# Attention weights of three query groups in four transposed by DMA, through one ring of three buffers

## The chip, the core and the metric

The kernel runs on one NeuronCore of a Trainium2 chip. The metric is the device time of one execution in microseconds (us), of which the median over several runs is given. The core's engines work through queues of their own and wait for each other by semaphores: PE (TensorE, matrix products), DVE (VectorE), ACT (ScalarE), POOL (GpSimd), and SP, which here only issues DMA transfers. PE's weight loads are a row of their own in the profile, PEld.

## What is computed

The input x is 4 sequences of 1024 tokens with 256 channels, in float32. Four layers are added to it in turn, each on its layer-normalized input: a linear recurrent layer, a sparse feed-forward layer with softmax gates and top-32 choices, an attention layer with 8 heads, and the same feed-forward layer once more. The change lies in the attention layer:

```python
q = (x @ Wq.T).reshape(b, t, N_HEADS, HEAD_DIM)           # 8 heads of 64
kv_latent = x @ Wkv_down.T                                # 64 wide, shared by the heads
k = (kv_latent @ Wk_up.T).reshape(b, t, N_HEADS, HEAD_DIM)
v = (kv_latent @ Wv_up.T).reshape(b, t, N_HEADS, HEAD_DIM)
scores = jnp.einsum('bqhd,bkhd->bhqk', q, k) * HEAD_DIM ** (-0.5)
attn = jax.nn.softmax(scores, axis=-1)
out = jnp.einsum('bhqk,bkhd->bqhd', attn, v)
return out.reshape(b, t, N_HEADS * HEAD_DIM) @ Wo.T
```

The key weights are folded into the queries and the value weights into the output, so that the kernel's attention works on the 64-wide latent itself.

## The kernel before

The program has three stages. The first, up to about 377 us, holds the recurrent layer, the head of the first feed-forward layer and its first eight tiles. The second, from about 377 to 1305 us, is the attention over all four sequences, with the other 24 tiles of the first feed-forward layer woven into it. The third is the second feed-forward layer.

In the second stage the method `heads` runs over units. A unit is a group of 128 queries (`q`, four of them in a block `nb` of 512) of a pair of heads (`g`, four pairs); there are 4 x 2 x 4 x 4 = 128 units, and each has two halves `j`, one for each head of the pair. I call one such half a "half": 256 in all. For each half,

- PE computes the scores of 128 queries against 1024 keys as four products (line 887) into one of two `sc` buffers in PSUM;
- DVE negates and copies them into one of four `pr` buffers, with the row's extreme value `nm` (line 893, and a small line 895 for units that go by DMA);
- ACT takes the exponentials in place and their sum `ssum` (line 896).

The weights then have to be turned, so that keys lie on the partitions. There are two ways. A unit "by DMA" (`by_dma`, before: `q` is 0 or 2) is split in two float16 parts in a `pd` buffer: ACT casts (line 899), POOL subtracts the cast from the original (line 900), and SP issues one DMA transpose of both parts (line 901) into a `d` buffer. A unit "by PE" (`q` is 1 or 3) takes eight PE transposes for each half (line 907) in two PSUM tiles, which ACT copies into a `p` buffer (line 912; in the last sequence DVE copies the first of the two, line 910).

Later `values_sum` multiplies the turned weights with the latent values (line 932): a unit by DMA takes 24 float16 products for each half (high and low parts of both factors), 48 in all, and a unit by PE 8 float32 products for each half, 16 in all, each of which the profile records as two. DVE makes the reciprocals `rs` of the sums (line 926), POOL spreads them over 64 columns for each head in `rows` (line 928), PE transposes that (line 940), ACT copies it (line 942) and DVE multiplies (line 943). Sums of units by DMA wait in the list `late`, those by PE in `pending`; both are emptied at the end of each sequence. The rings are: two `d` buffers for each half, one `p` buffer for each half, two `pd`, two `rows`.

The order on each engine is not that of the Python text alone. `merge` weaves the steps of the side work (queries, output products, the feed-forward tiles and others) between halves by due numbers written by hand, and then a scheduler orders each engine's queue, so that a sum can stand several halves behind the place where it was written. Nothing is reordered at run time: an instruction that waits holds up all that stand behind it on its engine.

A feed-forward tile of the second stage (`tile` with `fine=True`) writes exponentials into `ex` (ACT, line 615), finds the 32 largest of each of two gates by four rounds of top-8 search on DVE (line 674), and uses `ex` last in a POOL product with `xg` (line 658). It loads a precomputed product `full` by an SP transfer (line 599).

Of the kernel before, what the change touches and what calls it, by code (L numbers as in the profile page):

```python
# [10 lines left out]
F32 = mybir.dt.float32  # L11
# [3 lines left out]
F16 = mybir.dt.float16  # L15
# [6 lines left out]
P = 128  # L22
B = 4
T = 1024
D = 256
KD = D // P
TPB = T // P
# [3 lines left out]
HD = 64  # L31
PAIRS = HEADS // 2
# [147 lines left out]
class Banks:  # L180


    def __init__(self, pool, bufs):
        self.pool, self.bufs = pool, bufs
# [303 lines left out]
class Ffn:  # L488
# [100 lines left out]
    def tile(self, i, sp, psum, tags, out=None, fast=False, parts=None, tt=None, fine=False):  # L589


        nc, w = self.nc, self.w
        pool = nc.vector if fast else nc.gpsimd
        x = self.x[i]
        blk, tk = i // 4, slice((i % 4) * P, (i % 4 + 1) * P)
        full = None
        if blk in self.full:
            full = sp.tile([P, D], F32, tag="full", name="full")
            nc.sync.dma_start(full, self.full[blk][:, i % 4, :])
        pl = psum.tile([P, 2, D], tags[0], "pl")  # L600
        self.logits_product(pl, i)


        nr = TOPK // 8
        m8 = sp.tile([P, 2, nr, 8], F32, tag="m8", name="m8")
        e8 = sp.tile([P, 2, 8], F32, tag="e8", name="e8")
        nm = sp.tile([P, 2], F32, tag="nm", name="nm")
        ssum = sp.tile([P, 2], F32, tag="ssum", name="ssum")
        ex = sp.tile([P, 2, D], F32, tag="ex", name="ex")
        wk = sp.tile([P, 2, D], F32, tag="wk", name="wk", **({"bufs": 1} if fine else {}))  # L610
        for s in range(2):
            self.ordered(nc.vector.max, m8[:, s, 0, :], pl[:, s, :])
        nc.gpsimd.tensor_scalar(nm, m8[:, :, 0, 0], -1.0, 0.0, ALU.mult, ALU.add)
        for s in range(2):
            nc.scalar.activation(  # L615
                ex[:, s, :], pl[:, s, :], AF.Exp, bias=nm[:, s : s + 1], accum_out=ssum[:, s : s + 1]
            )
            self.last_exp = nc.scalar.activation(e8[:, s, :], m8[:, s, 0, :], AF.Exp, bias=nm[:, s : s + 1]).ins
        yield
        for r in range(nr):  # L620
            for s in range(2 if r else 0):
                self.ordered(nc.vector.max, m8[:, s, r, :], wk[:, s, :])
            for s in range(2):
                v, k = (wk, m8[:, s, r, :]) if r else (ex, e8[:, s, :])
                self.ordered(nc.vector.match_replace, wk[:, s, :], k, v[:, s, :], 0.0)
            if fine and r < nr - 1:
                yield
        pool.tensor_tensor(ex, ex, wk, ALU.subtract)  # L628
        rs = sp.tile([P, 2], F32, tag="rs", name="rs")
        nc.vector.reciprocal(rs, ssum)  # L630
        yield

        q = i % 4
        norm = self.norm[blk]
        if full is not None:
            nc.vector.scalar_tensor_tensor(full, full, rs[:, 0:1], ex[:, 0, :], ALU.mult, ALU.mult)
            ob = full
        else:
            if tt is not None:
                pf = psum.tile([P, D], tags[2], "pf")  # L640
                self.full_product(pf, tt, q)
            else:
                xn = sp.tile([P, D], F32, tag="fxn", name="fxn")
                with self.tc.issue_after(self.convolved):
                    nc.scalar.activation(
                        xn, x, AF.Identity, bias=norm[:, 1, q : q + 1], scale=norm[:, 0, q : q + 1]
                    )
                pf = self.product(sp, psum, tags, xn, None, parts)
            ob = sp.tile([P, D], F32, tag="ob", name="ob")
            nc.scalar.mul(ob, pf, rs[:, 0:1])  # L650
            pool.tensor_tensor(ob, ob, ex[:, 0, :], ALU.mult)
        yield

        xg = sp.tile([P, D], F32, tag="xg", name="xg", bufs=2)
        sc = sp.tile([P, 2], F32, tag="sc", name="sc")
        pool.tensor_scalar(sc, norm[:, :, q], rs[:, 1:2], 0.0, ALU.mult, ALU.add)
        nc.scalar.activation(xg, x, AF.Identity, bias=sc[:, 1:2], scale=sc[:, 0:1])
        pool.tensor_tensor(xg, xg, ex[:, 1, :], ALU.mult)
        nc.gpsimd.tensor_tensor(x, x, ob, ALU.add)
        pi = self.product(sp, psum, tags, xg, w.bias, parts)  # L660
        if out is None or fast:
            nc.vector.tensor_tensor(x, x, pi, ALU.add)
        else:
            yi = sp.tile([P, D], F32, tag="yi", name="yi")
            nc.scalar.copy(yi, pi)
            nc.gpsimd.tensor_tensor(x, x, yi, ALU.add)
        if out is not None:
            nc.sync.dma_start(out[i // 4][:, i % 4, :], x)
        yield
# [104 lines left out]
class Attention:  # L774
    def __init__(self, tc, x, ident, ident64, wqk, wvo, wd, sp, wp):
        self.nc, self.x, self.ident, self.ident64 = tc.nc, x, ident, ident64
        self.wqk, self.wvo, self.wd, self.sp, self.wp = wqk, wvo, wd, sp, wp
        self.hp = None
        self.k, self.xnt, self.qs, self.on = {}, {}, {}, {}

        self.sident = wp.tile([HD, HD], F32R, tag="sident", name="sident")
# [75 lines left out]
    def heads(self, b, psum):  # L857
# [2 lines left out]

        nc, sp, wp = self.nc, self.sp, self.hp
        kh, kl, la, lb = self.k[b]
        late, pending = [], []
        for nb, g, q in (
            (nb, g, q)
            for nb in range(2)
            for g in range(PAIRS)
            for q in ((0, 2, 1, 3) if b == B - 1 and nb and g == PAIRS - 1 else range(4))
        ):
            by_dma = q % 2 == 0  # L870
            if g == 0:
                self.on[b, nb, q] = wp.tile([P, PAIRS, P], F32, tag=f"on{q}", name=f"on{q}")
            qs = self.qs[b, nb, g]
            ssum = sp.tile([P, 2], F32, tag="ssum", name="ssum", bufs=4)
            if by_dma:
                pts = [wp.tile([P, 2 * TPB, P], F16, tag=f"d{j}", name=f"d{j}", bufs=2) for j in range(2)]
                parts = ((0, lb[0]), (TPB, lb[0]), (0, lb[1]))
                terms = [(v[:, c, :], i + c) for c in range(TPB) for i, v in parts]
            else:
                pts = [wp.tile([P, TPB, P], F32, tag=f"p{j}", name=f"p{j}") for j in range(2)]  # L880
                terms = [(la[:, c, :], c) for c in range(TPB)]
            for j in range(2):
                sc = psum.tile([P, T], "sc", "sc")
# [11 lines left out]
                    nc.vector.tensor_scalar(nm, nm, PSHIFT * math.log(2.0), None, ALU.add)  # L895
                nc.scalar.activation(pr, pr, AF.Exp, bias=nm, scale=-1.0, accum_out=ssum[:, j : j + 1])  # L896
                if by_dma:
                    pd = wp.tile([P, 2, T], F16, tag="pd", name="pd", bufs=2)
                    nc.scalar.copy(pd[:, 0, :], pr)  # L899
                    nc.gpsimd.tensor_tensor(pd[:, 1, :], pr, pd[:, 0, :], ALU.subtract)  # L900
                    nc.sync.dma_start_transpose(pts[j], pd.rearrange("p i k -> p (i k)"))
                else:
                    for half in range(2):
                        pt = psum.tile([P, 4, P], "t", "ptp")
                        for kk in range(4):
                            kc = 4 * half + kk
                            nc.tensor.transpose(pt[:, kk, :], pr[:, kc * P : (kc + 1) * P], self.ident)  # L907
                        dst = pts[j][:, 4 * half : 4 * half + 4, :]
                        if half == 0 and b == B - 1:
                            nc.vector.tensor_copy(dst, pt)  # L910
                        else:
                            nc.scalar.copy(dst, pt)  # L912
                if j == 0 and pending:
                    self.values_sum(*pending.pop(0), psum)
                if j == 1 and late and by_dma != (q > 0 and (b, nb, g) == (B - 1, 1, PAIRS - 1)):
                    self.values_sum(*late.pop(0), psum)
                yield
            (late if by_dma else pending).append((pts, terms, ssum, self.on[b, nb, q][:, g, :]))
        for args in late + pending:
            self.values_sum(*args, psum)  # L920

    def values_sum(self, pts, terms, ssum, on, psum):

        nc, sp = self.nc, self.sp
        rs = sp.tile([P, 2], F32, tag="rs", name="rs")
        nc.vector.reciprocal(rs, ssum)
        rows = sp.tile([P, 2, HD], F32, tag="rows", name="rows")
        nc.gpsimd.tensor_copy(rows, rs[:, :, None].to_broadcast([P, 2, HD]))  # L928
        po = psum.tile([P, 2, P], "s", "pmo")
        for n, (v, c) in enumerate(terms):  # L930
            for j in range(2):
# [4 lines left out]
                    start=(n == 0),  # L936
                    stop=(n == len(terms) - 1),
                )

        nc.tensor.transpose(po[:, 1, :], rows.rearrange("p j d -> p (j d)"), self.ident)  # L940
        rb = sp.tile([P, P], F32, tag="rb", name="rb", bufs=1)
        nc.scalar.copy(rb, po[:, 1, :])
        nc.vector.tensor_tensor(on, po[:, 0, :], rb, ALU.mult)
# [383 lines left out]
```

## Time and profile before

| | us |
|---|---|
| median of three runs | 1528.88 (1526.93 to 1530.15) |
| the profiled execution's own time | 1528.96 |
| its span, first to last instruction | 1527.2 |
| attention stage with scores (377 to 1287 us) | 910 |

| engine, 377 to 1287 us | busy us | share of 910 |
|---|---|---|
| PE | 819.72 | 90% |
| ACT | 708.19 | 78% |
| DVE | 696.12 | 76% |
| POOL | 427.61 | 47% |

A line of the profile that lists a group of instructions gives source line, engine, operation, the buffers written and read, their shapes and the count, then the time in which at least one of the group ran, the mean duration of one in ns, and the engine's idle time just before them with what ended it. A wait line says which instruction waited for which, the total in us, how often, and the longest. Issue instructions of DMA do not count as busy.

### The profile page before, as it was taken

To read this page: it belongs to the slowest core of one execution; us is meant where nothing else is said; L and a number is where in the kernel's file an instruction comes from. 1 tells how busy PE (TensorE), PEld (TensorE's weight loads), DVE (VectorE), ACT (ScalarE), POOL (GpSimd) and SP (SyncE) were. 2 spreads that over 40 slices of the span, in tenths; PEclk is the share of its full clock that TensorE was granted. 3 is DMA by queue.
4 is the path that set the end of the run, shared out by engine and by line. 5 is a ranking of instruction groups with operands and counts; after the bars stand their busy time and mean duration, and the time that the engine had idled before them with its cause. 6 is when DMAs were issued, how large, how long until landed. Compare 5 with 4: busy or idle time off the path is not lost.

```text
span 1527.2 us, 28862 instructions
## 1 busy us (share of the span) xinstructions
PE 1291.6 (85%) x10134; PEld 955.8 (63%) x10136; DVE 1194.9 (78%) x3938; ACT 1025.3 (67%) x2152; POOL 681.6 (45%) x849
## 2 busy tenths in 40 slices
PE   5879998697899888988888988889889999566766
PEld 3635455376677767756776766677777877344544
DVE  8976665697889777779778686877685775599998
ACT  5353433466889767887878777877777876566654
POOL 2033332162555444543544453444353544067775
PEclk9999999699999998999999899999999999679888
DMA  3010000321444343435344333534363445000000
GB/s 118 28 46 15 20 23 21 124 91 60 87 86 95 60 77 73 88 60 86 64 83 78 73 63 70 77 60 84 56 110 72 84 82 100 1 15 25 21 22 32
DMA packets 288612, 96.53 MB, mean 63 GB/s; under 512 B 268233, under 2 KB 284626, under 8 KB 288466
## 3 DMA queue, kind: packets, MB, share of 16 engines
q1 hardware_dynamic: 283024, 88.50, 28.9%
q10 hardware_dynamic: 5442, 6.18, 1.2%
q8 instruction: 80, 1.31, 0.3%
q14 instruction: 66, 0.54, 0.1%
HBM read 16.01 MB, written 11.53 MB: 18 GB/s over the span
## 4 chain that ended last, share of the span: by engine, by line
PE 34%; DVE 34%; ACT 16%; DMA 6%; issue 5%; POOL 4%; SPq 0%; ACTq 0%; POOLq 0%; DVEq 0%
DVE wk L674 8%; PE pmo L932 7%; DVE m L674 6%; PE sc L887 6%; DVE pr L893 6%; ACT pr L896 5%; DMA d<-pd 5%; PE po L437 3%; PE ptp L907 2%; ACT p L912 2%; ACT pd L899 2%; PE pmy L170 2%; PE pu L170 2%; DVE qs L854 2%; PE pz L452 1%
## 5 line engine op out<-in xcount | busy, mean ns | idle before, releaser
L900 POOL TENSOR_TENSOR pd<-pr,pd 128x1024 f16<-128x1024 f32 x128 | 274.3, 2145 | 196.0 <-ACT pd L899 152.1
L893 DVE TENSOR_SCALAR_CACHE_REDUCE pr<-sc 128x1024 f32<-128x1024 f32 x256 | 308.9, 1217 | 60.3 <-POOL pd L900 29.1
L896 ACT ACTIVATE pr<-pr,nm 128x1024 f32<-128x1024 f32 x256 | 294.5, 1152 | 57.2 <-DVE nm L895 38.8
L887 PE MATMUL sc<-kh,qs 128*128 128x512 f32 x512 | 184.4, 438 | 31.6 <-DVE pr L893 16.6
L907 PE MATMUL ptp<-ident,pr 128*128 128x128 f32 x1024 | 144.3, 277 | 24.7 <-ACT p L912 22.3
L887 PE MATMUL sc<-kl,qs 128*128 128x512 f32 x512 | 164.6, 401 | 0.0
L674 DVE MATCH_REPLACE8 wk<-m,wk 128x256 f32<-128x256 f32 x384 | 154.4, 405 | 0.1
L907 PEld LDWEIGHTS ptp<-ident,pr 128*128 128x128 f32 x1024 | 118.3, 142 | 54.2 <-ACT p L912 37.9
L674 DVE MAX8 m<-wk 128x8 f32<-128x256 f32 x384 | 149.9, 410 | 0.6
L912 ACT COPY p<-ptp 128x512 f32<-128x512 f32 x224 | 123.5, 587 | 40.0 <-PE pmo L932 29.8
L899 ACT CAST pd<-pr 128x1024 f16<-128x1024 f32 x128 | 133.6, 1046 | 24.8 <-DMA d<-pd 23.7
L932 PE MATMUL pmo<-p,la 128*64 128x128 f32 x2048 | 136.5, 284 | 4.3 <-DVE qs L854 2.9
L932 PEld LDWEIGHTS pmo<-p,la 128*64 128x64 f32 x2048 | 117.8, 141 | 23.1 <-issue 4.5
L887 PEld LDWEIGHTS sc<-kh,qs 128*128 128x128 f32 x512 | 85.4, 195 | 58.4 <-DVE pr L893 25.4
L628 POOL TENSOR_TENSOR ex<-ex,wk 128x512 f32<-128x512 f32 x61 | 77.9, 1277 | 79.8 <-DVE wk L674 64.9
L887 PEld LDWEIGHTS sc<-kl,qs 128*128 128x128 f32 x512 | 97.3, 191 | 22.7 <-issue 1.0
L932 PE MATMUL pmo<-d,lb 128*64 128x128 f16 x3072 | 101.6, 222 | 7.7 <-ACT ex L615 5.0
L932 PEld LDWEIGHTS <-lb 128*64 128x64 f16 x3072 | 91.4, 111 | 22.2 <-issue 19.0
L928 POOL COPY rows<-rs 128x128 f32<-128x128 f32 x128 | 37.3, 294 | 140.3 <-PE pmo L940 135.6
L699 PE MATMUL pf<-wf,vt 128*128 128x256 f32 x288 | 83.5, 432 | 4.4 <-ACT vt L697 3.6
L147 PE MATMUL pt<-ident,xn 128*128 128x128 f32 x256 | 50.0, 318 | 41.6 <-ACT xn L145 32.9
L556 PE MATMUL pl<-lint,xc_f 128*128 128x512 f32 x128 | 71.8, 648 | 10.4 <-ACT xc_f L587 10.4
(308 smaller groups left out, 2769.9 us busy)
## 6 DMA issues: line engine op xcount, KB each, us to landing
tt<-ft SPq DMA_DIRECT2D x16, 256.0 KB
tt<-tt SPq DMA_DIRECT2D x8, 512.0 KB
out<-x SPq DMA_DIRECT2D x32, 128.0 KB
x<-in_x ACTq DMA_DIRECT2D x6, 512.0 KB
pf<-pfs SPq DMA_DIRECT2D x12, 256.0 KB
full<-pf SPq DMA_DIRECT2D x24, 128.0 KB
d<-pd SPq DMA_TRANSPOSE x128
wa<-in_w_attn SPq DMA_DIRECT2D x2, 640.0 KB
```

Source lines behind the costliest of these rows:

```text
L556: self.last_logits = nc.tensor.matmul(v, x, w.lint, start=False, stop=True).ins
L628: pool.tensor_tensor(ex, ex, wk, ALU.subtract)
L674: ins = make(*args).ins
L699: nc.tensor.matmul(dst, vt[:, k, :], w.wf[:, k, :], start=(k == 0 and bias is None), stop=(k == KD - 1))
L887: nc.tensor.matmul(sc[:, sl], qs[:, j, q * P : (q + 1) * P], kk[:, sl], start=(i == 0), stop=(i == 1))
L893: nc.vector.tensor_scalar(pr, sc, -1.0, FMAX, ALU.mult, ALU.min, accum_out=nm)
L896: nc.scalar.activation(pr, pr, AF.Exp, bias=nm, scale=-1.0, accum_out=ssum[:, j : j + 1])
L899: nc.scalar.copy(pd[:, 0, :], pr)
L900: nc.gpsimd.tensor_tensor(pd[:, 1, :], pr, pd[:, 0, :], ALU.subtract)
L907: nc.tensor.transpose(pt[:, kk, :], pr[:, kc * P : (kc + 1) * P], self.ident)
L912: nc.scalar.copy(dst, pt)
L932: nc.tensor.matmul(po[j * HD : (j + 1) * HD, 0, :], v, pts[j][:, c, :], start=(n == 0), stop=(n == len(terms) - 1),)
```

## The change

Units with `q` 0, 1 and 2 go by DMA and only `q` 3 by PE, except in the last four units of all, which stay as they were. That makes 95 units by DMA and 33 by PE, against 64 and 64. The `d` and `p` buffers become one ring of three for each half, used by both kinds, the `pd` ring gets a third buffer, and to make room the woven feed-forward tiles keep one `ex` and one `xg` instead of two. There is one list `due` in place of `late` and `pending`: the sum of a unit is written at the second half of the second next unit, for both kinds, and the list is carried over from one sequence to the next. The reciprocals are taken a half earlier, and `rows` with its transpose is replaced by two products with the identity, whose stationary operand is one column of `rs` read 64 times.

```diff
@@ tile
-        ex = sp.tile([P, 2, D], F32, tag="ex", name="ex")
+        ex = sp.tile([P, 2, D], F32, tag="ex", name="ex", **({"bufs": 1} if fine else {}))
...
-        xg = sp.tile([P, D], F32, tag="xg", name="xg", bufs=2)
+        xg = sp.tile([P, D], F32, tag="xg", name="xg", bufs=1 if fine else 2)
@@ heads
-            by_dma = q % 2 == 0
+            by_dma = q % 2 == 0 if (b, nb, g) == (B - 1, 1, PAIRS - 1) else q < 3
...
-            ssum = sp.tile([P, 2], F32, tag="ssum", name="ssum", bufs=4)
+            ssum = sp.tile([P, 2], F32, tag="ssum", name="ssum", bufs=6)
+            pts = [wp.tile([P, TPB, P], F32, tag=f"p{j}", name=f"p{j}", bufs=3) for j in range(2)]
             if by_dma:
-                pts = [wp.tile([P, 2 * TPB, P], F16, tag=f"d{j}", name=f"d{j}", bufs=2) for j in range(2)]
+                pts = [t.bitcast(F16).rearrange("p c (i q) -> p (c i) q", i=2) for t in pts]
...
-                pts = [wp.tile([P, TPB, P], F32, tag=f"p{j}", name=f"p{j}") for j in range(2)]
...
-                    pd = wp.tile([P, 2, T], F16, tag="pd", name="pd", bufs=2)
+                    pd = wp.tile([P, 2, T], F16, tag="pd", name="pd", bufs=3)
...
-                if j == 0 and pending:
-                    self.values_sum(*pending.pop(0), psum)
-                if j == 1 and late and by_dma != (q > 0 and (b, nb, g) == (B - 1, 1, PAIRS - 1)):
-                    self.values_sum(*late.pop(0), psum)
+                if j == 0 and len(self.due) > 1:
+                    rs = self.reciprocals(self.due[0][2])
+                if j == 1 and len(self.due) > 1:
+                    self.values_sum(*self.due.pop(0), rs, psum)
                 yield
-            (late if by_dma else pending).append((pts, terms, ssum, self.on[b, nb, q][:, g, :]))
-        for args in late + pending:
-            self.values_sum(*args, psum)
+            self.due.append((pts, terms, ssum, self.on[b, nb, q][:, g, :]))
+        if b == B - 1:
+            for unit in self.due:
+                self.values_sum(*unit, self.reciprocals(unit[2]), psum)
@@ values_sum
-        rs = sp.tile([P, 2], F32, tag="rs", name="rs")
-        nc.vector.reciprocal(rs, ssum)
-        rows = sp.tile([P, 2, HD], F32, tag="rows", name="rows")
-        nc.gpsimd.tensor_copy(rows, rs[:, :, None].to_broadcast([P, 2, HD]))
...
-        nc.tensor.transpose(po[:, 1, :], rows.rearrange("p j d -> p (j d)"), self.ident)
+        for j in range(2):
+            nc.tensor.matmul(
+                po[j * HD : (j + 1) * HD, 1, :],
+                rs[:, j : j + 1].to_broadcast([P, HD]),
+                self.ident,
+                start=True,
+                stop=True,
+            )
```

More of the change, by code (lines that the diff above doesn't have):

```diff
@@ L778, in __init__ @@
         self.hp = None
+        self.due = []
         self.k, self.xnt, self.qs, self.on = {}, {}, {}, {}
@@ L862, in heads @@
         kh, kl, la, lb = self.k[b]
-        late, pending = [], []
         for nb, g, q in (
@@ L912, in heads, with reciprocals, values_sum @@
                             nc.scalar.copy(dst, pt)
-                if j == 0 and pending:
-                    self.values_sum(*pending.pop(0), psum)
-                if j == 1 and late and by_dma != (q > 0 and (b, nb, g) == (B - 1, 1, PAIRS - 1)):
-                    self.values_sum(*late.pop(0), psum)
+                if j == 0 and len(self.due) > 1:
+                    rs = self.reciprocals(self.due[0][2])
+                if j == 1 and len(self.due) > 1:
+                    self.values_sum(*self.due.pop(0), rs, psum)
                 yield
-            (late if by_dma else pending).append((pts, terms, ssum, self.on[b, nb, q][:, g, :]))
-        for args in late + pending:
-            self.values_sum(*args, psum)
-    def values_sum(self, pts, terms, ssum, on, psum):
+            self.due.append((pts, terms, ssum, self.on[b, nb, q][:, g, :]))
+        if b == B - 1:
+            for unit in self.due:
+                self.values_sum(*unit, self.reciprocals(unit[2]), psum)
+    def reciprocals(self, ssum):
         nc, sp = self.nc, self.sp
-        rs = sp.tile([P, 2], F32, tag="rs", name="rs")
+        rs = sp.tile([P, 2], F32, tag="rs", name="rs", bufs=4)
         nc.vector.reciprocal(rs, ssum)
-        rows = sp.tile([P, 2, HD], F32, tag="rows", name="rows")
-        nc.gpsimd.tensor_copy(rows, rs[:, :, None].to_broadcast([P, 2, HD]))
+        return rs
+    def values_sum(self, pts, terms, ssum, on, rs, psum):
+        nc, sp = self.nc, self.sp
         po = psum.tile([P, 2, P], "s", "pmo")
```

## The prediction

> **What bounds the kernel now.** I read the page first (shares and groups), then the stretch of the attention stage, the chain of waits there, the wait lists, and last the timeline around one transpose. All changed units lie between 377 and 1287 us.
>
> ```profile
> 377.00:1287.00 910.00, 819.72 (x8184) 650.42 (x8185) 696.12 (x1966) 708.19 (x1363) 427.61 (x417) 0.98 0.43 77
> 1100.00:1287.00 187.00, 178.71 (x1911) 145.32 (x1911) 136.29 (x333) 148.22 (x259) 87.30 (x73) 0.99 0.48 87
> ```
>
> The columns are length, then busy us of PE, PEld, DVE, ACT and POOL, the granted clock and the DMA share. PE is the fullest engine (90%; 96% in the last sequence), but ACT (78%) and DVE (76%) are close. PE's work is 819.7 / 256 = 3.20 us a half, the pace 910 / 256 = 3.55.
>
> ```profile
> L900 POOL TENSOR_TENSOR pd<-pr,pd 128x1024 f16<-128x1024 f32 x128 | 274.3, 2145 | 196.0 <-ACT pd L899 152.1
> L907 PE MATMUL ptp<-ident,pr 128*128 128x128 f32 x1024 | 144.3, 277 | 24.7 <-ACT p L912 22.3
> L932 PE MATMUL pmo<-p,la 128*64 128x128 f32 x2048 | 136.5, 284 | 4.3 <-DVE qs L854 2.9
> L912 ACT COPY p<-ptp 128x512 f32<-128x512 f32 x224 | 123.5, 587 | 40.0 <-PE pmo L932 29.8
> L899 ACT CAST pd<-pr 128x1024 f16<-128x1024 f32 x128 | 133.6, 1046 | 24.8 <-DMA d<-pd 23.7
> L932 PE MATMUL pmo<-d,lb 128*64 128x128 f16 x3072 | 101.6, 222 | 7.7 <-ACT ex L615 5.0
> L928 POOL COPY rows<-rs 128x128 f32<-128x128 f32 x128 | 37.3, 294 | 140.3 <-PE pmo L940 135.6
> ```
>
> These are what the edit trades. A unit by PE costs PE (144.3 + 136.5) / 64 = 4.39 us, a unit by DMA 101.6 / 64 = 1.59. The idle column shows the two ring waits: copies wait for an older sum to free `p`, casts for an older transpose to free `pd`.
>
> ```profile
> 485.03 1.53 PE L932 MATMUL pmo<-d,lb 128*64 128x128 f16 x48
> 486.62 4.54 SPq L901 DMA_TRANSPOSE d<-pd  x2
> 491.19 1.05 ACT L899 CAST pd<-pr 128x1024 f16<-128x1024 f32 x1 [0.33 <-DMA d<-pd]
> 492.32 2.14 POOL L900 TENSOR_TENSOR pd<-pr,pd 128x1024 f16<-128x1024 f32 x1 [0.56 <-ACT pd L899]
> 495.77 1.21 DVE L893 TENSOR_SCALAR_CACHE_REDUCE pr<-sc 128x1024 f32<-128x1024 f32 x1
> ```
>
> This is one turn of a loop that the change tightens. A sum ends (486.56), the transpose into the buffer it freed is issued at once, 4.57 us later ACT casts into the `pd` that this released, POOL subtracts and frees a `pr`, DVE reduces into it and so frees an `sc` for PE. The shortest turn is 1.53 + 4.57 + 1.05 + 0.08 + 2.14 + 1.29 + about 1.0 for four score products = 11.7 us.
>
> **The change, part by part.**
>
> *Units moved.* 31 units go from PE to DMA. PE: 31 x (1.59 - 4.39) = -87 us of work. ACT: 62 casts at 1.046 = +65; copies fall from 224 to 114 at 0.587 = -65; nothing. DVE: 62 small additions (line 895 takes 0.145) = +9; copies of the last sequence from 32 to 18 at 0.687 = -10; nothing. POOL: 62 subtractions at 2.145 = +133. SP: 62 issues at about 2 us; SP has nothing else dense. DMA: two transposes issued back to back begin 1.9 to 2.6 us apart and the share is 0.43 for 128 of them, so about 0.64 for 190: room, though the second of a pair lands up to 2.6 us later.
>
> *`rows` gone.* POOL -37 us; its 135.6 us of waiting there held up no subtraction that I can find (a subtraction starts within 0.14 us of its cast in three cases of four), so I take nothing for it. On PE a transpose (eight take 1.04 us in the timeline, 0.13 each) gives way to two float32 products of 64 columns. The nearest row is line 932 on `la`: sixteen such products take 1.97 us, 0.123 each, so 0.246 a unit. 128 x (0.246 - 0.13) = +15 us; the other end is +5, since weight loads sit idle 10 us on "issue" ahead of line 940 and that may vanish. I take +15. PE in sum: -72, to 748 us, 2.92 a half.
>
> *One `ex`, one `xg`.* The next tile's exponential waits for `nm` from POOL (line 613), which in the new order too stands behind the last product that reads the old `ex` (line 658). That wait covers it: 0; without it, up to 0.77 us (line 658) for 24 tiles.
>
> *Reciprocals earlier, lists carried over.* Same 128 instructions; ACT and DVE behind them see no new wait; the sums at the end of a sequence were spread by the scheduler already: 0.
>
> *POOL beside DVE.* The row first: line 636, which has two inputs in SBUF, takes 0.477 us at best and 1.054 at the median, and single ones of the tiny line 66 take up to 2.16 instead of 0.16, when a POOL operation runs. I add such excess over all DVE forms in the stage: 38 us for 428 us of POOL. With 427.6 + 133 - 37 = 524 it would be 47, so +9 on DVE. The Trainium skill's page "SBUF — State Buffer", section "Who interferes with whom", says that a DVE instruction with two SBUF inputs blocks fully against a GpSimd instruction that reads SBUF. By the rule, the stage's some 154 such instructions (24 on line 636, the rest in the normalizations) meet a subtraction with POOL's share and wait half of it: 154 x 0.47 x 1.07 = 77 before, 95 after, +18. The trace has half of the rule's amount, so I take +9, of which about 3 lie on the path (DVE holds 250 of the chain's 928 us).
>
> *The rings.* Here the change adds waits. In the written order of both programs a sum stands well behind its unit: by DMA 9.4 halves behind before, 9.3 after. The destination comes round after 4 units (8 halves) before, but after 3 units (6 halves) now, so a transpose waits longer for its buffer on SP, with all later transposes and `full` loads behind it, and the casts on ACT wait for the transpose, with exponentials and copies behind them. I compared, for each cast, how many halves' exponentials ACT has issued before it with how many halves' scores PE has before the gating sum. At a lead of zero or less the trace has 26 casts that idled 19.4 us in sum (0.75 each); at one, 0.12; at two, 0.09. In the new order 73 of 181 casts have no lead (before 26 of 122): 63 us of ACT waiting against 25, +38. For copies into `p` the same count goes from 100 at 0.36 to 62: -14.
>
> Seen as pace: the turn of 11.7 us spans at most 4 halves 41 times in the new order, 10 times in the old. Laid end to end over the 256 halves, 27 turns over 101 halves (3.74 each) bind in the new order, 2 in the old. At PE's own pace 3.74 halves take 10.9 us. With turns of 12.2 us (the shortest and half a us of queueing) that is 27 x 1.3 = +35 us.
>
> **The sum, made twice.** (A) By the fullest engine: PE 748 + turns 35 + the 90 us that PE idles now, less 12 of waits for ACT's copies that go with half of them, plus 14 because ACT and DVE become fuller, + 3 for the port = 878, against 910: -32. (B) By the chain: PE's chain pieces are 321 of its 820 us, so -72 counts 0.39: -28; + 38 - 14 on ACT, + 3: -1. I trust neither more and take the middle, -16. The profiled execution's 1528.96 us (span 1527.2 and 1.76 around it, within 0.1 us of the median of the runs) becomes 1513.
>
> **Rivals.**
>
> *The ring turns set the pace (slower).* Place: ACT's casts. A turn that holds the second transpose of a pair costs 11.7 + 2.6 = 14.3 us; then 27 x (14.3 - 10.9) = 92, and 748 + 92 + 95 = 935, +25: 1554. It decides from turns of 13.4 us up, where 748 + 27 x 2.5 + 95 reaches 910. For it: the turn in the timeline above took about 13.0 with its scores, and SP already waits longest for sums:
>
> ```profile
> SPq L901 <- PE pmo L932: 363.1, 52, 16.1
> ```
>
> Against it: in the old order the tightest turns mostly ran beside PE work, and ACT lost only 23.7 us.
>
> *PE alone counts.* If the old rings' waits were what PE's idle time came from and new ones hide, all of -72 shows: 1457. For it: the last sequence, at 96%. Against it: only 35% of the chain lies on PE.
>
> *ACT and DVE carry it.* Their work doesn't change; if they set the pace with today's waits, nothing moves: 1529.
>
> *The edit isn't what it says.* Sums written two units later stand 4.6 units later in the queue, so the ring of three is tighter than the words; that is counted above.
>
> **Numbers.** Forecast, a gain of 4 to 40 us: 0.42, its own range 1489 to 1525. PE alone, a gain above 40: 0.10. No change within 0.2% (3 us, about what a measurement of this kernel can tell): 0.06. Ring turns: 0.34; other slower ends (port at 18 and the new products dearer, SP blocked by a `full` load): 0.08. So faster 0.52, same 0.06, slower 0.42. The range of 8 in 10 reaches from 1474 (a gain of 55, between A and PE alone) to 1560 (the ring case and a little).
>
> **What would show it.** Right: PE busy in the stage near 748 us, line 932 on `p` with `la` near 70 us, POOL near 524; casts waiting for DMA 50 to 70 us in some 75 places; the stage some 895 us long. Wrong: casts waiting over 90 us, or DVE's line 893 waiting for POOL's line 900 well over the present 29 (the ring case); PE idle still 90 us or less (PE alone); line 945 far from 0.25 us a unit.

## The result, and the profile after

| | us | ratio to before, 95% interval |
|---|---|---|
| before, median of five runs | 1528.12 (1526.93 to 1530.15) | 1 |
| the changed kernel, median of five runs | 1568.93 (1566.66 to 1574.03) | 1.027 (1.025 to 1.029) |
| predicted | 1513 (1474 to 1560) | |

The change made the kernel 41 us slower, where a gain of 16 was forecast. The profiled execution took 1570.18 us, its span is 1568.5. The first and the third stage differ from before by less than 5 us; the loss lies in the attention stage.

Busy time of the stage after, and of its last sequence (length; then PE, PEld, DVE, ACT, POOL; granted clock; DMA share):

```profile
378.84:1330.77 951.93, 780.16 (x8554) 603.34 (x8560) 715.89 (x2014) 714.78 (x1316) 524.99 (x354) 0.95 0.53 109
1144.00:1331.00 187.00, 165.47 (x1934) 130.35 (x1933) 122.30 (x320) 148.43 (x253) 105.47 (x54) 0.96 0.65 128
```

The stage is 42 us longer than the 910 of before. PE has 40 us less to do (72 were foreseen) and POOL 97 more (96 were foreseen), but PE now idles 172 us instead of 90, and its granted clock is 0.95 instead of 0.98. The last sequence, where PE was 96% busy, has PE at 88%, and its scores take 209 us from first to last instead of 202. The groups that answer to those of before (busy, mean ns of one, idle before it and who ended it):

```profile
L900 POOL TENSOR_TENSOR pd<-pr,pd 128x1024 f16<-128x1024 f32 x190 | 406.1, 2144 | 268.4 <-ACT pd L899 243.4
L899 ACT CAST pd<-pr 128x1024 f16<-128x1024 f32 x190 | 197.0, 1041 | 48.4 <-DMA p<-pd 47.7
L936 PE MATMUL pmo<-p,lb 128*64 128x128 f16 x4560 | 158.8, 227 | 18.1 <-ACT ex L615 7.3
L907 PE MATMUL ptp<-ident,pr 128*128 128x128 f32 x528 | 77.3, 286 | 21.1 <-ACT pr L896 10.5
L936 PE MATMUL pmo<-p,la 128*64 128x128 f32 x1056 | 69.9, 288 | 9.7 <-DVE qs L855 8.6
L945 PE MATMUL pmo<-ident,rs 128*64 128x128 f32 x496 | 50.9, 277 | 0.0
```

The work moved as planned: transposes and sums fell from 382.4 to 306.0 us. Casts wait twice as long for transposes as before (47.7 against 23.7). The stage's wait list (total, times, longest) tells who is held up behind them:

```profile
DVE pr L893 <- POOL pd L900: 52.1, 44, 2.9
ACT pd L899 <- DMA p<-pd: 47.7, 41, 3.5
PE sc L887 <- DVE pr L893: 38.5, 46, 2.0
PE sc L887 <- DVE qs L855: 32.5, 23, 5.1
DVE rs L927 <- PE pmo L945: 24.9, 25, 3.6
```

Read from below: reciprocals wait until column products free an `rs`; scores wait for queries (before 14.1 us) and for reductions (16.6), which wait for subtractions (29.1). These waits overlap along one chain and must not be added. The chain that ended last is lost in this trace ahead of about 1242 us, so the stage's causes had to come from runs.

### The profile page after: what moved, and what is told of

Its sections match the earlier page's. It is cut to its first block, busy times and chain, and to the rows that moved or that the text cites. A ratio compares the mean times of both kernels' runs of the same rounds, so it can differ in the third digit from the quotient of the medians.

```text
span 1568.5 us, 29955 instructions
## 1 busy us (share of the span) xinstructions
PE 1252.3 (80%) x10513; PEld 908.6 (58%) x10520; DVE 1215.0 (77%) x3986; ACT 1031.9 (66%) x2104; POOL 778.5 (50%) x783
## 3 DMA queue, kind: packets, MB, share of 16 engines
q1 hardware_dynamic: 411984, 121.01, 35.1%
## 5 line engine op out<-in xcount | busy, mean ns | idle before, releaser
L900 POOL TENSOR_TENSOR pd<-pr,pd 128x1024 f16<-128x1024 f32 x190 | 406.1, 2144 | 268.4 <-ACT pd L899 243.4
L893 DVE TENSOR_SCALAR_CACHE_REDUCE pr<-sc 128x1024 f32<-128x1024 f32 x256 | 309.9, 1218 | 87.9 <-POOL pd L900 52.1
L899 ACT CAST pd<-pr 128x1024 f16<-128x1024 f32 x190 | 197.0, 1041 | 48.4 <-DMA p<-pd 47.7
L936 PE MATMUL pmo<-p,lb 128*64 128x128 f16 x4560 | 158.8, 227 | 18.1 <-ACT ex L615 7.3
L936 PEld LDWEIGHTS <-lb 128*64 128x64 f16 x4560 | 142.5, 115 | 47.3 <-issue 40.7
L628 POOL TENSOR_TENSOR ex<-ex,wk 128x512 f32<-128x512 f32 x61 | 77.8, 1275 | 85.8 <-DVE wk L674 60.8
L907 PE MATMUL ptp<-ident,pr 128*128 128x128 f32 x528 | 77.3, 286 | 21.1 <-ACT pr L896 10.5
L907 PEld LDWEIGHTS ptp<-ident,pr 128*128 128x128 f32 x528 | 61.0, 145 | 37.8 <-ACT pr L896 16.0
L936 PE MATMUL pmo<-p,la 128*64 128x128 f32 x1056 | 69.9, 288 | 9.7 <-DVE qs L855 8.6
L615 ACT ACTIVATE ex<-pl,nm 128x256 f32<-128x256 f32 x128 | 60.0, 470 | 26.2 <-POOL nm L613 25.8
L699 PEld LDWEIGHTS pf<-wf,vt 128*128 128x128 f32 x288 | 59.1, 214 | 30.2 <-ACT vt L697 12.8
L147 PEld LDWEIGHTS pt<-ident,xn 128*128 128x128 f32 x256 | 33.1, 158 | 70.1 <-ACT xn L145 28.0
```

Source lines behind the costliest of these rows:

```text
L147: nc.tensor.transpose(pt[:, k, i * P : (i + 1) * P], xn[:, k * P : (k + 1) * P], ident)
L699: nc.tensor.matmul(dst, vt[:, k, :], w.wf[:, k, :], start=(k == 0 and bias is None), stop=(k == KD - 1))
L893: nc.vector.tensor_scalar(pr, sc, -1.0, FMAX, ALU.mult, ALU.min, accum_out=nm)
L936: nc.tensor.matmul(po[j * HD : (j + 1) * HD, 0, :], v, pts[j][:, c, :], start=(n == 0), stop=(n == len(terms) - 1),)
```

## The experiments

All ratios are to the kernel before, run on the same chip. Where it says that the order is fixed, issue-order edges between each instruction and the next on its engine keep the queues of the named kernel; they add no wait. (In the trace of the kernel before, VectorE's 3170 instructions start in the order of the program, so the queues that are fixed are the ones that run.)

### One part undone, or one part alone

More `rs` buffers, `bufs=4` to `bufs=8`:

> The changed kernel with the buffers of `rs` doubled from 4 to 8: VectorE's reciprocal no longer waits for the column products of line 945, nothing else is different. Theory R (reciprocals: VectorE stands 24.9 us behind that wait, with reductions queued behind it, and this is where the loss comes from): 1545 us, 20 to 30 below the changed kernel's 1568.9. Theory T (turns of the ring set the pace: casts, subtractions and reductions wait for transposes, and these for sums): the reciprocal's wait only shows time that would be lost anyway; 1563 to 1569, at most 6 us gained, and the waits of reductions for subtractions (51.2) stay or grow.

1611.07 us, ratio 1.0531 (1.0507 to 1.0556): slower by another 42 us. Neither theory said so. Its trace gave the clue: the transposes moved the same packets, but q1's share of the DMA engines rose. Four more small buffers, 32 bytes a partition each, had shifted everything behind them by 128 bytes, the rings from 0 to 128 modulo 512.

Two groups by DMA, the rest of the change kept:

```diff
-            by_dma = q % 2 == 0 if (b, nb, g) == (B - 1, 1, PAIRS - 1) else q < 3
+            by_dma = q % 2 == 0
```

> The changed kernel with two of four groups by DMA again; the ring of three, three `pd`, sums at the second next unit, early reciprocals and column products stay. Theory T (the third group overfills the ring): casts without a lead are 28 of 121 in the written order, as before the change (26 of 122), so the waits go and the time is within 10 us of before: 1519 to 1535. Theory L (the lists, the one ring or the reciprocals cost the time): still 1550 or more.

1582.79 us, 1.0341 (1.0314 to 1.0367). My theory missed by 48 us or more: without the third group the rest of the change is 14 us slower than the whole.

The third group alone, in the kernel before:

```diff
-            by_dma = q % 2 == 0
+            by_dma = q % 2 == 0 if (b, nb, g) == (B - 1, 1, PAIRS - 1) else q < 3
```

> The kernel before with only the third group sent by DMA: its own rings (two destinations and two `pd` for DMA units, one for PE units), its own two lists and `rows` stay. 69 of 184 casts have no lead. Theory T: casts and reductions wait as in the changed kernel, 1555 to 1585; with two `pd` rather more than less. Theory L: PE's saving shows, 1500 to 1525.

1580.92 us, 1.0336 (1.0317 to 1.0356); casts waited 107.4 us. As the theory of turns says. As they stand, each half of the change alone costs more than both together; but the buffers of this kernel lie at 384 modulo 512 and those of the other two at 0, and that is worth 34 us here, as a run below shows.

The column products alone:

```diff
-        rows = sp.tile([P, 2, HD], F32, tag="rows", name="rows")
-        nc.gpsimd.tensor_copy(rows, rs[:, :, None].to_broadcast([P, 2, HD]))
...
-        nc.tensor.transpose(po[:, 1, :], rows.rearrange("p j d -> p (j d)"), self.ident)
+        for j in range(2):
+            nc.tensor.matmul(
+                po[j * HD : (j + 1) * HD, 1, :],
+                rs[:, j : j + 1].to_broadcast([P, HD]),
...
```

> The kernel before with only the copy into `rows` and its transpose replaced by the two column products. POOL loses 37 us of copies, PE exchanges a transpose of 0.13 us for two products. The prediction's term: 0.246 us a unit, +15 us of PE work, and a third to all of it in the time: 1533 to 1544. The rival: weight loads stood idle ahead of the transpose and the products come without that, so 1523 to 1530.

1546.99 us, 1.0109 (1.0086 to 1.0133), 3 us above the first case: it costs 16 us. The scheduler made a new order for it, so not all of that is the products' own.

### Where the buffers lie

```diff
-        nc, sp, wp = self.nc, self.sp, self.hp
+        nc, sp, wp = self.nc, self.sp, self.hp; pad = wp.tile([P, 32], F32, tag="pad", name="pad") if b == 0 else None
```

This line in the changed kernel ([P, 32] of float32 is 128 bytes a partition):

> The changed kernel with one unused buffer of 128 bytes a partition ahead of the rings, so that `p` and `pd` begin at 128 instead of 0 modulo 512 bytes; no instruction and no order differs. In the run with eight `rs` buffers the same shift had come about by itself, its transposes' packets of 256 bytes took 23.4 ns instead of 19.9, the last packet landed 4.08 us after the issue instead of 3.41, and the kernel took 1611 us. Theory A (where the buffers lie sets the transposes' time, and the turns of the ring pass it on): 1600 to 1615. Theory O (that run was slow for its other order of instructions): 1566 to 1575.

1595.91 us, 1.0428 (1.0387 to 1.047). With not one instruction moved in any queue, the kernel is 27 us slower, as theory A says. The transposes' queue and the casts' waits, first in the changed kernel:

```profile
q1 hardware_dynamic: 411984, 121.01, 35.1%
ACT pd L899 <- DMA p<-pd: 47.7, 41, 3.5
```

and in the shifted one:

```profile
q1 hardware_dynamic: 411984, 121.01, 39.9%
ACT pd L899 <- DMA p<-pd: 85.8, 67, 3.3
```

The packets and bytes are the same, their time is not. Casts, exponentials and subtractions take as long as before the shift (the 190 subtractions 407 us in sum in both traces), so of the rings' own work it is the transposes that the shift slows. Eight `rs` buffers, shifted back by 384 more bytes:

> Eight `rs` buffers in the changed kernel, with 384 unused bytes that bring `p` and `pd` back to 0 modulo 512; the order is that of the first run with eight `rs`. Theory A: the reciprocal's wait alone is seen, 1545 to 1570. Theory O: 1605 or more.

1575.19 us, 1.03 (1.0265 to 1.0335). This is 36 us below the first run with eight `rs`, in the same order: theory A, though 5 us above its range. The reciprocals' wait for column products is gone from this trace, and nothing was gained; the reciprocals now wait for exponentials:

```profile
DVE rs L927 <- ACT pr L896: 43.8, 39, 2.9
```

The changed kernel has 15.9 us there. A wait of 25 us had been worth nothing: it stood in front of another.

The 128 bytes in the kernel before:

> The kernel before with 128 unused bytes ahead of its rings, which moves `d`, `p` and `pd` from 384 to 0 modulo 512; the order is unchanged. Theory A: transposes land some 0.6 us earlier; before has few tight turns (26 casts without a lead), so 1512 to 1525, a small gain. Theory O: 1528 to 1532.

1523.41 us, 0.9964 (0.9952 to 0.9976). A small gain, within theory A's range, and the fastest kernel with the full result in this study; casts waited 11.6 us instead of 23.7.

The third group alone, with the same line:

> The kernel before with the third group alone and 128 unused bytes, so that `d`, `p` and `pd` lie at 0 modulo 512 (they lay at 384 in the run of 1580.9, in the same order of instructions). Landings come 0.6 us earlier. By the slope of this order, 48 us for landings 1.33 us earlier: about 1558. If its turns stop binding at once: 1535 to 1548. If the place of the buffers only mattered in the ring of three: 1575 to 1583.

1546.62 us, 1.0119 (1.0104 to 1.0134), 34 us less than unshifted, in the range of the second case, though casts still waited 59.9 us in 66 places. An unshifted repeat gave 1580.15 us (1.0335, 1.03 to 1.037):

> The third group alone in the old rings, run once more as a control for the chip (the very kernel of the first run, not shifted): 1576 to 1585 by every theory.

### Shorter turns

```diff
-                    nc.gpsimd.tensor_tensor(pd[:, 1, :], pr, pd[:, 0, :], ALU.subtract)
-                    nc.sync.dma_start_transpose(pts[j], pd.rearrange("p i k -> p (i k)"))
+                    nc.gpsimd.tensor_tensor(pd[:, 0, :], pr, pd[:, 0, :], ALU.subtract)
+                    nc.sync.dma_start_transpose(pts[j][:, 0:TPB, :], pd[:, 0, :])
```

> The changed kernel with its order of instructions fixed and only one of the two parts transposed (1024 columns instead of 2048): POOL subtracts in place, the transposes carry that part alone, and the products read it twice, so the output lacks the high part; every engine keeps its instructions and their durations, only a turn of the ring is some 1 us shorter. From the shifted kernel to the changed one, landings 0.67 us earlier gave 27 us. Theory T (ring turns hold PE up): 1568.9 less 25 to 45, so 1524 to 1544, and casts hardly wait for DMA. Rival C (the lists, column products and POOL's load hold the time, the ring is only where it is seen): at most 12 us gained, 1557 to 1569.

1557.19 us, 1.0182 (1.0147 to 1.0217): rival C by its figure, 12 us gained; theory T missed by 13 us. Casts wait less than a third of what they did, yet reductions still wait for subtractions and scores for queries:

```profile
DVE pr L893 <- POOL pd L900: 48.4, 46, 2.9
PE sc L887 <- DVE pr L893: 37.7, 44, 2.1
PE sc L887 <- DVE qs L855: 27.3, 22, 3.7
ACT pd L899 <- DMA p<-pd: 14.9, 19, 2.3
```

> The same in the kernel before with the third group alone (1580.9 with both parts; unshifted buffers, casts waiting 107 us for DMA). Theory T: the whole loss and PE's saving come back, 1490 to 1520, below the kernel before. Rival C, or a rival that moved units cost something else, POOL's 133 us or the port: 1540 or more.

1533.18 us, 1.0037 (1.0023 to 1.0051), 48 us less. That lies between the ranges: most of the loss came back, PE's saving did not, and the kernel is still 17 us above the run that follows, its like with two groups.

> The same in the kernel before, in its own order, as the base for the other two. Few turns bind there, so theory T expects a gain of 5 to 15 us: 1513 to 1523. If short transposes help every kernel alike (rival), 25 to 45 us here too: 1483 to 1503.

1516.41 us, 0.991 (0.9878 to 0.9942): 12 us less, as theory T says. In these three runs the transposes also move half the bytes (their queue's share falls from 35.1% to 20.5% in the changed kernel), so a lighter load of the DMA engines comes with the shorter turn and was not told apart from it.

The three orders side by side. Landing is the mean time from the start of an issue to the end of that transpose's 256-byte packets in the trace, good to some 0.1 us:

| order | landing, us: time, us |
|---|---|
| before | 3.93: 1528.1; 3.36: 1523.4; 2.69: 1516.4 |
| third group alone | 3.94: 1580.9; 3.35: 1546.6; 2.61: 1533.2 |
| changed kernel | 4.09: 1595.9; 3.41: 1568.9; 2.41: 1557.2 |

A microsecond of landing is worth 8 to 10 us in the order of before, 58 and then 18 in that of the third group, 40 and then 12 in that of the changed kernel. This fits turns that bind: the slope is steep where the forecast counted many of them, and it flattens as casts wait less. The number of turns itself was not measured.

### Which part of the rest

Column products in the places of the old transposes, in the fixed order of before, with eight `rs` and `d`, `p` and `pd` at their old place modulo 512:

> The kernel before with the column products in the places where the transposes of `rows` stood, the order of all queues fixed to that of before, eight `rs` buffers, and unused bytes that keep `d`, `p` and `pd` at 384 modulo 512. Free of any new order it cost 17 us. If the two products themselves cost it (0.246 us a unit against 0.13 on a PE that is 90% full): 1536 to 1546. If the scheduler's other order or the reciprocals' new wait cost it: 1526 to 1534; from the last product ahead of them to the product after them takes 0.37 us in the changed kernel and 0.315 with the transpose, so 7 us of PE work, of which some 3 on the path.

1540.14 us, 1.0081 (1.0048 to 1.0113). With the order kept, the operation costs 12 us. PE's busy time in the stage rises from 818.2 to 825.6.

In the kernel with two groups by DMA, `rows` and its transpose put back (with one `rows` buffer instead of the two of before):

> Two of four groups by DMA as before, with the one ring of three, the later sums and three `pd`, but `rows` and its transpose back in place of the column products; buffers at 0 modulo 512 as in the run with the column products (1582.8). If the column products hold the 55 us (POOL's copy frees an `rs` at once, a product only after the whole sum): 1525 to 1545. If the ring and the later sums hold it: 1560 to 1575, 12 to 20 us off for the products' own cost.

1550.29 us, 1.0142 (1.0127 to 1.0157), between the two cases: 32 us less than with column products, and still 27 above the kernel before with its buffers as well placed. Against that kernel (the run with 128 bytes),

```profile
PE sc L887 <- DVE qs L854: 13.4, 12, 4.3
DVE on L943 <- ACT rb L942: 50.8, 41, 4.7
```

this one has

```profile
PE sc L887 <- DVE qs L855: 34.6, 18, 4.5
DVE on L949 <- ACT rb L948: 75.4, 45, 4.7
```

Casts wait about as little in one as in the other (13.3 and 11.6 us). What grew is the scores' wait for queries at the start of a block, and VectorE's wait in the last step of a sum, which stands ahead of reductions and query subtractions in its queue. The lone `ex` shows no wait of its own: ACT waits 4.6 us for line 613 in one kernel and 4.3 in the other.

> The changed kernel with `rows` and its transpose back, buffers at 0 modulo 512 as in the changed kernel. POOL gets 37 us of copies again. By the products' own cost, measured at 12 us in a fixed order: 1552 to 1562. If the freeing of `rs` matters too: 1535 to 1552. If POOL is by now the tighter engine, the copies stand in the way of subtractions: 1569 or more.

1557.42 us, 1.0196 (1.0179 to 1.0213), in the first case: 11.5 us less than the changed kernel, by the products' own cost.

Each sum written one unit earlier:

```diff
-                if j == 0 and len(self.due) > 1:
+                if j == 0 and self.due:
...
-                if j == 1 and len(self.due) > 1:
+                if j == 1 and self.due:
```

> The changed kernel with each sum written at the next unit instead of the second next; the ring of three stays. Casts without a lead fall from 73 to 36 of 181. If the later sums cost the time (ring turns, and less PE work that stands ready where the scores wait for queries): 1535 to 1555. If sums that come earlier wait for their own transposes instead: 1562 to 1580.

1568.18 us, 1.0265 (1.025 to 1.028), no difference, in the range of the second case; but its cause, sums that wait for their own transposes, is not in the trace (4.3 us in 6 places). Waiting casts fell from 47.7 to 33.7 us and nothing came of it.

### How much PE work counts

```diff
-                        nc.tensor.matmul(
+                        (i or kb) or nc.tensor.matmul(sc[:, sl], qs[:, j, q * P : (q + 1) * P], kk[:, sl], start=True, stop=True); nc.tensor.matmul(
```

> The kernel before with the first of each half's four score products issued twice (0.23 us each, 256 of them, 59 us of PE work more), every queue otherwise in the order of before and with the same waits. If PE work counts with the 0.39 that the chain gave: 1528 plus 23, 1551. If PE is the bound: 1575 to 1587. If PE work hides in waits: under 1540.

1552.16 us, 1.0145 (1.0119 to 1.017), the first case.

> The same 59 us added to the changed kernel, in its order. If PE work counts there as in the kernel before: 1569 plus as much as the run beside it gains, 1590 or more. If PE waits for the other engines there, and the added work only fills stretches in which the clock had fallen to half (90 us of the stage): 1560 to 1577, with less time at half clock.

1572.95 us, 1.029 (1.027 to 1.0311), the second case. The two stages, before with the added work first:

```profile
380.72:1312.07 931.35, 864.69 (x8435) 693.10 (x8435) 696.97 (x1967) 710.02 (x1365) 428.13 (x417) 0.98 0.43 76
379.46:1336.11 956.65, 824.02 (x8827) 645.61 (x8831) 722.26 (x2018) 715.81 (x1318) 526.91 (x355) 0.96 0.53 108
```

The same 59 us cost 24 us in the kernel before and 4 in the changed one, where the interval of the difference reaches from about 0 to 8. PE's work counts with 0.41 there and with some 0.07 here. The clock explains little of that: time at half clock in the stage fell from 90.4 to 69.3 us with the work added (before: 42.3 to 32.1), which gives back about 7 us of PE's work here and 5 there (half of the fall of busy time at half clock). What work *taken from* PE brings in the kernel before was not run; it need not count as much as work added.

## Why the prediction was wrong, step by step

Four kernels with the buffers at 0 modulo 512 make a staircase from before to after (the kernel before took 1527.7 to 1528.3 us beside them, and by the intervals a difference is good to 2 to 4 us):

| step | us | difference |
|---|---|---|
| before | 1528.1 | |
| buffers at 0 modulo 512 (the change brings this along) | 1523.4 | -5 |
| one ring of three, one list, three `pd`, one `ex` and `xg`, earlier reciprocals, one `rows` | 1550.3 | +27 |
| third group by DMA | 1557.4 | +7 |
| column products in place of `rows` | 1568.9 | +12 |

The forecast's -16, the middle of sums A and B, splits the same way: units moved, rings and port -27; column products +10; lists, single buffers and reciprocals 0; the place of the buffers 0. Measured: +7, +12, +27 and -5. So of the 57 us between forecast and result, 34 lie in the first term and 27 in the third. The split holds for this sequence of steps: on the old rings the third group alone came to +23 with its buffers at 0 modulo 512.

- **PE's saving, the step that carried the sign.** Sum A took all of -72 us and kept the 90 us that PE idled; PE idles 172. Sum B took 0.39 of -72. That share was right for work added to the kernel before (0.41). It was wrong to carry it over: in the changed kernel, where PE idles for 172 us of the stage, its work counts 0.07. At 0.07 the 87 us of the units are worth 6; with the 12 us that shorter turns still bring in the changed kernel, that would make +6, near the +7 (an estimate from two other runs, not a test).
- **PE's busy time, 748 foreseen, 780 measured.** The units fell by 76 instead of 87. Two terms were missing. Busy time isn't additive: 59 us of added work raised it by 46.5 and 43.9, or by some 51 in both with the clock's change taken out, and by that rate -72 would show as -62. And PE was busy for 67.4 us at half clock instead of 39.8, which is 14 us of work lost. These two leave about 9 of the 32 us unexplained.
- **Lists, one `ex`, one `xg`: 0 foreseen, +27 measured** together with the shared ring. Here a term was put at nothing on the ground that each edit alone was covered, and what the new order of sums does to others was not asked. In the changed kernel the later sums by themselves are not it (run with sums at the next unit). Which of the ring, the list and the single buffers it is stays open; the waits that grew are the scores' for queries (13.4 to 34.6 us) and VectorE's for `rb` (50.8 to 75.4). The order of before on the new ring was not run, so a worse order by the scheduler is a rival that stands.
- **Reciprocals, "no new wait": false, but free.** The wait came, 24.9 us in 25 places, and the kernel without it (eight `rs`, in an order of its own) was 6 us slower.
- **Column products.** 15 us of PE work foreseen; 7 measured in busy time in the fixed order, 12 in the kernel's time. The row of line 945 has 0.41 us a unit (50.9 for 124 units), far from 0.25, which the prediction called a sign of being wrong; but the transpose that went has 0.33 by its row in the kernel before, not 0.13:

```profile
L940 PE MATMUL pmo<-ident,rows 128*128 128x128 f32 x128 | 42.6, 333 | 0.0
```

Rows overlap with the work beside them, so neither is a cost. In the kernel with two groups by DMA the products cost 32, for which the runs give no reason.

- **Rings.** The mechanism was right, and its price came out near, in part by luck. I foresaw 63 us of waiting casts in 73 places for transposes as they landed before; with transposes landing like that (the shifted kernel) it is 85.8 in 67. From there to turns that hardly bind is 1595.9 to 1557.2, 39 us, where the sum had 35 or 38. So a third more waiting cost as much as foreseen, and the last 12 of the 39 come from runs that also halve the transposes' bytes. What I couldn't see is that the new layout takes 27 of these back; with it casts waited 47.7 us in 41 places, below the 50 to 70 in some 75 that were forecast.
- **POOL, ACT.** POOL 524 us as foreseen. ACT +7, DVE +20, where nothing was foreseen but the port. By the same count as before (durations over each form's lower level) the excess on DVE rose from 38 to 53 us: +15, between the trace's +9 and the rule's +18. That is no support for either: with `rows` back in the changed kernel POOL was busier still (555.4 us), and DVE's busy time was 695.9, against 696.1 before. In this case the excess goes with the order, not with POOL's busy time alone; line 636 takes 40.4 us in sum in the changed kernel, 26.2 in that one and 28.3 before.
- **Rivals.** The ring rival had the side and came nearest (1554), and one of its two signs came true: reductions waited 52.1 us for subtractions instead of 29. The other did not: casts waited 47.7 us, not over 90. "PE alone counts" fell with PE's idle time of 172 us and with the run that added work. "ACT and DVE carry it" is nearest to what holds PE up in the changed kernel, but their waits grew, and the time with them.

## The half clock

The granted clock's steps in the traces last 3.413 us or a multiple of it, but for at most one a trace. Here is the changed kernel in steps of that length (columns as above), and PE in the same stretch:

```profile
857.00:860.40 3.40, 1.75 (x52) 1.51 (x51) 3.16 (x9) 2.89 (x7) 1.31 (x1) 1.00 0.14 33
860.40:863.80 3.40, 1.16 (x9) 1.07 (x9) 3.34 (x12) 2.88 (x6) 2.29 (x2) 1.00 1.23 275
863.80:867.20 3.40, 0.26 (x2) 0.00 (x0) 3.40 (x16) 2.76 (x5) 0.08 (x1) 0.51 0.00 1
867.20:870.60 3.40, 2.10 (x7) 1.33 (x7) 2.44 (x8) 1.52 (x3) 1.23 (x1) 0.50 0.01 2
870.60:874.10 3.50, 3.39 (x28) 3.07 (x30) 3.01 (x3) 0.64 (x2) 3.50 (x4) 0.50 0.00 0
874.10:877.50 3.40, 3.40 (x61) 2.69 (x58) 0.88 (x3) 0.85 (x2) 0.17 (x1) 1.00 0.65 160
```

```profile
862.64 0.51 PE L887 MATMUL sc<-kh,qs 128*128 128x512 f32 x1 [3.68 <-DVE qs L855]
868.32 1.08 PE L147 MATMUL pt<-ident,xn 128*128 128x128 f32 x4 [4.26 <-DVE qs L855]
871.33 3.29 PE L936 MATMUL pmo<-p,la 128*64 128x128 f32 x32
```

PE waits 3.68 us for queries and is busy for 1.16 of 3.4 us; the next window runs at half clock, stays there through a window that is 62% busy, and the sum on `la` takes 3.29 us for 32 records instead of 1.97. Only after a window that is 97% busy does the clock return. Over the traces of before, after and the third group alone, full-clock windows with PE busy below 40% were followed by half clock 68 times in 68, from 40 to 50% 25 times in 43, from 50 to 60% 6 in 69, above that 5 in 960. From half clock none of 86 windows below 80% led back; above 90% 95 of 96 did. The Trainium skill, page "TensorE: Matmul & The Clock Gate", section "HAM oscillation — how this bites in real kernels", speaks of idle gaps over some 3.4 us. That fits the stretch above, but of the 104 full-clock windows that led to half clock 34 had no single gap of PE as long as 2 us; short gaps among short work suffice. I had priced PE's idle time as time only, not as slower work after it. What the half clock costs the kernel as a whole no run shows.

## What to carry to other kernels

Before you count a saved engine's work, ask whether that engine will still set the pace once the saving is in: add a known amount of its work to both kernels, in a fixed order, and the two differences tell. A ring's price can be read as the slope of the time over the length of its turn, and a change of layout can lengthen or shorten every turn without moving an instruction, so compare addresses before you compare orders. A wait in a list is worth what its removal brings, which was nothing for 25 us here, and an edit priced at nothing needs a run of its own.

## What I had not expected of the hardware

**256 bytes.** At 384 or 128 modulo 512, which is 128 past a multiple of 256, the transposes' packets of 256 bytes took 22.95 ns on average (before) and 23.46 (shifted); at 0 modulo 512 they took 19.88 and 19.91, and landings came 0.6 to 0.7 us sooner. The Trainium skill, page "DMA: Bandwidth & Descriptors", section "How a descriptor splits into AXI transactions", says that a transaction must start at an address aligned to 256 bytes and that bytes ahead of the start are fetched all the same. By that page's beats of 32 bytes, an estimate, 8 beats become 12, half more for every packet. Measured, the mean rises by 15 to 18%, and not evenly: at 0 modulo 512, 98 or 99 packets in 100 take 18 ns or less, at the other places 79 or 80. So the place of the buffers is shown to be the cause, but not that it acts by this rule. Whether the source or the destination matters was not tried.
